# Key eviction per head, 128-wide transposes and reordered statistics in a fused window-attention and Fourier kernel; its constants loaded by fewer transfers on another queue

## The chip, the core and the metric

The kernel runs on one core of a Trainium2 chip. A core has five engines with an instruction queue each. TensorE multiplies matrices (PE in the profile; its loads of the stationary operand are a row of their own, PEld). VectorE (DVE) and ScalarE (ACT) work element by element and can read PSUM, the eight accumulator banks of 2 KB per partition into which TensorE writes. GpSimd (POOL) works on SBUF only. SyncE (SP) issues transfers; ScalarE can issue them too, from the same queue as its arithmetic. Engines wait for each other through semaphores, and each engine takes its instructions strictly in order.

The metric is the device time of one execution in microseconds (us); the median of several runs is compared.

## The reference

Input `x` is 32 images of 56x56 tokens with 128 channels, float32. Two layers are added to it one after the other.

```
x = x + attention(group_norm(x))          # shifted 7x7 windows, 4 heads of 32 channels
x = x + feed_forward(fourier(group_norm(x)))
attention:  q,k,v = win @ w_qkv.T;  softmax(q k^T * scale + bias[h] + mask) v;  @ w_proj.T + b_proj
            bias[h, i, j] = rpb_table[rel_index(i, j), h]      # 49 x 49 per head
fourier:    DCT along one image axis, 32 modes kept, a 128x128 product per mode, inverse DCT;
            the same along the other axis with other weights; the two are added
feed_forward: relu(h @ W1 + b1) @ W2 + b2, 512 hidden channels
```

An image is 8x8 windows of 49 tokens. The windows of one row of windows (392 tokens) are called a row here; there are 256 rows.

## The kernel before

Everything is one software pipeline over **cycles**, one per row, 273 in all. In a cycle, row r starts attention, row r-1 has its softmax divided, row r-2 is transposed, multiplied by its values and projected, and the image before goes through one stage of the Fourier layer or the feed-forward. The order of all work of PE, ACT, DVE and POOL in the loop is written out by hand (the scheduler is off there); the instructions before it, which load constants, are placed by the scheduler. The stage functions of a cycle are called in this order: `full_first`, then `quarters` and `half_columns` (either one first), `eighths`, `full_last`.

In `full_first`, PE transposes the softmax of row r-2 (`attn_transpose`, L393: 8 transposes of 113x113 into two PSUM banks, which DVE copies out at L403 and ACT at L401). Then `attn_qk` makes the queries (L307) and the keys (L312) of row r. ACT evicts the queries (L308). The scores matmul works on two heads at once and needs two copies of the keys: `k_sb[0]` with the channels of the odd heads zero, `k_sb[1]` with those of the even heads zero. ACT writes the first from the keys' bank (L314) and DVE the second (L317); each multiplies by a column of `heads`, ones and zeros per channel, and adds a bias. ACT then squares the row r-3 (L478) and DVE sums it (L480). The feed-forward in (`ff_in`, L670) writes four hidden blocks into four PSUM banks, and ACT evicts them with the ReLU (L678).

PSUM is two pools of four banks: `pa` for attention, `pc` for Fourier and feed-forward. A matmul that takes a bank waits for the eviction of what was there. In four of eight cycles `modes_transpose` (L606, evicted by DVE at L612) takes two `pc` banks just ahead of `ff_in`, whose last two blocks then wait for a bank.

`quarters` has the scores (L347; DVE adds bias and mask at L356) and the inverse transforms (L627). `attn_max` (DVE L366, POOL L367) subtracts the row maximum; ACT takes the exponential later (L373). `eighths` has the values (L415; evicted by ACT L446 and DVE L444). `full_last` has the feed-forward out (L690; DVE L699), the load of three rows of the next image (`image_group`: L243, ACT L253, DVE L254) and the projection (L455; DVE L463). By the row's number within its image, cycles 0 to 7 differ in what Fourier does: row 2 has the statistics (`fourier_stats`: DVE L490 and L498, PE L502, POOL L520) and the width transform (L548, ACT L555), rows 3 and 4 the height transform, row 5 a mix of modes (L585) and no feed-forward, rows 6, 7, 0 and 1 the inverse transforms; all but row 5 have one group of feed-forward.

Ahead of the loop, ACT's queue issues 50 transfers of constants, among them 25 of the 49 rows of the relative position bias `rpb` (L152). SP's queue issues the image, the other 24 rows and one copy of `rpb` onto partitions 64 and up (L153). DVE adds `rpb` and the mask into `bm` (L170), which L356 reads.

Of the kernel before, what the change touches and what calls it, by code (L numbers as in the profile page):

```python
# [15 lines left out]
P = 128  # L16
S = 56
# [31 lines left out]
def swin_fourier_kernel(  # L49
# [68 lines left out]

    def const_load(shape, src, name):
        t = const.tile(shape, F32, tag=name, name=name)  # L120
        nc.scalar.dma_start(t, src)
        return t
# [17 lines left out]
    rpb = const.tile([P, NH, WS, WS], F32, tag="rpb", name="rpb")  # L140
    nc.vector.memset(rpb, 0.0)
    span = 2 * WS - 1
    with nc.allow_non_contiguous_dma(reason="relative position bias, once"):
        for i in range(WT):
            iy, ix = divmod(i, WS)
            src = bass.AP(
                rpb_rev.tensor,
                rpb_rev.offset + (WS - 1 - iy) * span + WS - 1 - ix,
                [[span * span, NH], [span, WS], [1, WS]],
            )  # L150
            eng = nc.sync if i % 2 else nc.scalar
            eng.dma_start(rpb[i : i + 1], src.unsqueeze(0))  # L152
# [4 lines left out]
    for hh in range(2):  # L157
        rows = slice(hh * JP, hh * JP + WT)
        for k, src in enumerate((shift_mask[:, 0, 0:WT], shift_mask[:, 2, JP : JP + WT])):
            nc.scalar.dma_start(mask_sb[rows, :, k], src.rearrange("r p j -> p r j"))  # L160
# [18 lines left out]
    for r in range(0, TC, S):  # L179
        nc.scalar.dma_start(dct_h[r : r + S - SS], dct[r + SS : r + S])  # L180
        nc.scalar.dma_start(dct_h[r + S - SS : r + S], dct[r : r + SS])
# [3 lines left out]
    with nc.allow_non_contiguous_dma(reason="constant, once"):  # L185
        for li, ls in enumerate(HALVES):
            nc.scalar.dma_start(idctw[ls], idct_w[ls, li * 2 * S : (li + 1) * 2 * S])
            src = idct_h.rearrange("p (h r) -> p h r", r=4)[ls, :, 2 * li : 2 * li + 2]
            nc.scalar.dma_start(idcth[ls, : S - SS], src[:, SS:])
            nc.scalar.dma_start(idcth[ls, S - SS :], src[:, :SS])  # L190
# [15 lines left out]

    k_sb = [big.tile([P, NWR, WT], F32, tag=f"k{u}", name=f"k{u}") for u in range(2)]
    heads = const.tile([P, 2], F32, tag="heads", name="heads")
    nc.vector.memset(heads, 0.0)
    for h in range(NH):  # L210
        nc.vector.memset(heads[h * HD : (h + 1) * HD, h % 2 : h % 2 + 1], 1.0)
# [50 lines left out]
    def image_norm(im):  # L262
# [33 lines left out]
        im.bias = small.tile([P, 5], F32, tag="bqkv", name="bqkv")  # L296
        nc.vector.tensor_scalar(im.bias[:, 0:1], pb[:, 0:1], QS, None, ALU.mult)
        nc.vector.tensor_copy(im.bias[:, 1:3], pb[:, 1:3])
        nc.vector.tensor_scalar(im.bias[:, 3:5], heads, im.bias[:, 1:2], None, ALU.mult)
# [3 lines left out]
    def attn_qk(im, i):  # L303

        q, src = q_sb, im.xw[i][:, :RT]
        pq = attn_bank()
        nc.tensor.matmul(pq[:, :RT], lhsT=im.w[:, 0:C], rhs=src, start=True, stop=True)  # L307
        nc.scalar.activation(  # L308
            q[:, :RT], pq[:, :RT], AF.Identity, bias=im.bias[:, 0:1], scale=QS
        )  # L310
        pk = attn_bank()
        nc.tensor.matmul(pk[:, :RT], lhsT=im.w[:, C : 2 * C], rhs=src, start=True, stop=True)  # L312
        pk3 = pk[:, :RT].rearrange("p (w j) -> p w j", j=WT)
        nc.scalar.activation(  # L314
            k_sb[0], pk3, AF.Identity, bias=im.bias[:, 3:4], scale=heads[:, 0:1]
        )
        nc.vector.tensor_scalar(  # L317
            k_sb[1], pk3, heads[:, 1:2], im.bias[:, 4:5], ALU.mult, ALU.add
        )
# [65 lines left out]
    def attn_transpose(im, i, r):  # L385

        a = a_sb[r % 3]
        im.aT = []
        for hf in range(2):
            pt = attn_bank()  # L390
            for m in range(4):
                pr, hp = 2 * hf + m // 2, m % 2
                nc.tensor.transpose(  # L393
                    pt[:PW, m * P : m * P + PW],
                    a[:PW, hp, 2 * pr : 2 * pr + 2].rearrange("p w j -> p (w j)")[:, :PW],
                    ident[:PW, :PW],
                )
            aT = work.tile([P, 4, P], F32, tag="aT", name="aT")
            src = pt[:PW].rearrange("p (m x) -> p m x", x=P)[:, :, :PW]
            if hf:  # L400
                nc.scalar.copy(aT[:PW, :, :PW], src)  # L401
            else:
                nc.vector.tensor_copy(aT[:PW, :, :PW], src)  # L403
            im.aT.append(aT)

    def attn_values(im, i, r):
# [4 lines left out]
        for pr in range(NWR // 2):  # L411
            for h in range(NH):
                for u in range(2):
# [4 lines left out]
                        rhs=im.aT[pr // 2][  # L418
                            ks, 2 * (pr % 2) + h // 2, h % 2 * JP : h % 2 * JP + WT
                        ],  # L420
# [325 lines left out]
    def full_first(cycle, norm):  # L746
# [13 lines left out]
        for im, c in fourier(cycle):  # L760
            if c == 0:
# [5 lines left out]
        for im, c in fourier(cycle):  # L767
            if c in FF_AT:
                ff_in(im, FF_AT.index(c))
        for im, c in fourier(cycle):  # L770
            if c == 0:
                next(im.stats)
# [23 lines left out]
    def quarters(cycle):  # L796
# [3 lines left out]
        for im, c in fourier(cycle):  # L800
            for width, g in back_groups(c):
                modes_back(im, width, g)

# [28 lines left out]
    with tc.manual_schedule(engines={ET.PE, ET.Activation, ET.DVE, ET.Pool}):  # L832
# [6 lines left out]
        for cycle in range(NB * NWR + CONV_BEGIN + FF_AT[-1] - NWR + 1):  # L839
            full_first(cycle, norm)  # L840
            if cycle >= CONV_BEGIN and (cycle - CONV_BEGIN) % NWR != 3:
                quarters(cycle)
                if row(cycle)[0]:
                    attn_max(cycle)
                half_columns(cycle)
                eighths(cycle)
            else:
                half_columns(cycle)
                quarters(cycle)
                eighths(cycle)  # L850
                if row(cycle)[0]:
                    attn_max(cycle)
# [68 lines left out]
```

## Time and profile before

| what | value |
|---|---|
| median of 3 runs | 4120.96 us (4119.18 to 4123.46) |
| the profiled execution | 4120.96 us, its span 4119.1 us |
| mean granted TensorE clock | 0.986 |
| PE busy | 3897.2 us (95%) |
| PEld busy | 3193.5 us (78%) |
| DVE busy | 2336.8 us (57%) |
| ACT busy | 2150.4 us (52%) |
| POOL busy | 1367.1 us (33%) |
| first queries matmul (L307) starts | at 63.62 us |
| DMA engines busy, first 63.6 us | 60% |

The span runs from the first to the last instruction. Busy times are unions per engine; a busy PE is not PE at its peak, since matmuls overlap. A group's row gives line, engine, operation, what it writes and reads, sizes and count, then busy time and the mean of one in ns, then the engine's idle time ahead of it and what ended it. In a timeline a row is: start, length, engine, line, operation, tiles, count, and in brackets the idle time ahead with the releaser. A queue (ACTq, SPq) is the engine issuing a transfer.

### The profile page before, as it was taken

What the parts mean: (1) busy time and instruction counts of PE and PEld (TensorE: products, weight loads), DVE (VectorE), ACT (ScalarE), POOL (GpSimd) and SP (SyncE); (2) the same over time, 40 slices, a digit from 0 to 9 for tenths busy, and PEclk for the clock granted to TensorE, in tenths of its full rate; (3) what the DMA queues carried; (4) which work ended last, traced back from release to release, by engine and by line L of the source; (5) the groups of instructions that cost most, each with busy time, mean ns of one, the idle gap of its engine ahead of it and who ended that gap; (6) DMA issues with size and microseconds to landing.
All of it is one profiled execution on the core that took longest, in us unless ns stands there. A gap on an engine that the chain in (4) does not pass through costs nothing.

```text
span 4119.1 us, 165389 instructions
## 1 busy us (share of the span) xinstructions
PE 3897.2 (95%) x74816; PEld 3193.5 (78%) x74816; DVE 2336.8 (57%) x4859; ACT 2150.4 (52%) x3809; POOL 1367.1 (33%) x1357
## 2 busy tenths in 40 slices
PE   3799999999999999999999999999999999999999
PEld 2577877878777787788777878778778787777887
DVE  3565555665555656555655555565555655556551
ACT  1355555555555555555555555555555555555553
POOL 2333333333333333333333333333333333333321
PEclk9899999999999999999999999999999999999999
DMA  3211222221222221222212222212222212222122
GB/s 90 54 50 51 66 74 75 73 64 47 73 73 74 75 56 54 74 70 77 75 52 57 71 71 78 69 51 61 72 75 73 64 46 73 74 73 75 48 61 62
DMA packets 533828, 273.06 MB, mean 66 GB/s; under 512 B 29795, under 2 KB 532740, under 8 KB 532868
## 3 DMA queue, kind: packets, MB, share of 16 engines
q1 hardware_dynamic: 522072, 257.04, 23.7%
q8 instruction: 588, 9.63, 0.9%
q10 hardware_dynamic: 11052, 5.44, 0.6%
q14 instruction: 116, 0.95, 0.1%
HBM read 159.60 MB, written 102.76 MB: 64 GB/s over the span
## 4 chain that ended last, share of the span: by engine, by line
PE 86%; DVE 6%; ACT 3%; POOL 1%; issue 1%; ACTq 1%; DMA 0%; POOLq 0%; DVEq 0%
PE pc L690 18%; PE pc L670 14%; PE pa L347 7%; PE pa L327 6%; PE pc L585 6%; PE pc L548 5%; PE pa L393 5%; PE pa L415 4%; PE pc L627 4%; PE pa L455 4%; PE pa L307 4%; PE pa L312 4%; PE pc L606 2%; PE pa L243 2%; POOL a L367 1%
## 5 line engine op out<-in xcount | busy, mean ns | idle before, releaser
L381 POOL TENSOR_TENSOR a<-a,rs 128x784 f32<-128x784 f32 x256 | 389.5, 1522 | 1624.3 <-DVE rs L380 1397.2
L690 PE MATMUL pc<-wff,hid 128*128 128x128 f32 (+1 forms) x6400 | 778.8, 279 | 2.0 <-ACT oT L446 0.9
L690 PEld LDWEIGHTS pc<-wff,hid 128*128 128x128 f32 (+1 forms) x6400 | 731.3, 189 | 22.2 <-issue 3.2
L670 PE MATMUL pc<-xf,wff 128*128 128x512 f32 (+2 forms) x1792 | 730.6, 545 | 8.7 <-ACT hid L678 6.4
L678 ACT ACTIVATE hid<-pc,b1sb 128x512 f32<-128x512 f32 (+2 forms) x896 | 559.2, 633 | 181.3 <-PE pc L670 172.5
L670 PEld LDWEIGHTS pc<-xf,wff 128*128 128x128 f32 x1792 | 320.7, 190 | 311.1 <-issue 197.9
L367 POOL TENSOR_TENSOR a<-a,mx 128x784 f32<-128x784 f32 x256 | 388.8, 1519 | 422.5 <-DVE mx L366 409.4
L699 DVE TENSOR_TENSOR res<-pc,res 128x512 f32<-128x512 f32 (+2 forms) x256 | 143.5, 571 | 588.6 <-issue 288.1
L401 ACT COPY aT<-pa 113x452 f32<-113x452 f32 x256 | 138.4, 541 | 547.7 <-PE pa L393 547.7
L317 DVE TENSOR_SCALAR k<-pa,heads,bqkv 128x392 f32<-128x392 f32 x256 | 175.4, 685 | 433.5 <-ACT k L314 433.5
L258 POOL TENSOR_TENSOR xl<-xl,bproj 112x384 f32<-112x384 f32 (+1 forms) x256 | 291.1, 1138 | 291.1 <-PE pa L243 286.3
L347 PEld LDWEIGHTS pa<-k,q 64*64 64x64 f32 x16384 | 266.4, 135 | 131.6 <-issue 58.9
L373 ACT ACTIVATE a<-a 128x784 f32<-128x784 f32 x256 | 221.4, 865 | 253.5 <-POOL a L367 253.5
L356 DVE TENSOR_TENSOR a<-pa,bm 128x392 f32<-128x392 f32 x512 | 260.2, 551 | 162.5 <-PE pa L347 162.2
L444 DVE TENSOR_SCALAR oT<-pa,bqkv 128x147 f32<-128x147 f32 (+2 forms) x768 | 171.2, 280 | 300.3 <-PE pa L415 300.3
L393 PE MATMUL pa<-ident,a 113*113 113x113 f32 x2048 | 259.4, 271 | 84.7 <-ACT xw L253 83.9
L334 ACT COPY v<-pa 128x512 f32<-128x512 f32 x256 | 152.7, 597 | 340.8 <-PE pa L327 340.8
L347 PE MATMUL pa<-k,q 64*64 64x49 f32 x16384 | 300.0, 221 | 10.4 <-ACT k L314 6.2
L393 PEld LDWEIGHTS pa<-ident,a 113*113 113x113 f32 x2048 | 234.2, 185 | 90.9 <-issue 86.6
L660 POOL TENSOR_TENSOR res<-res,b2sb 128x512 f32<-128x512 f32 (+2 forms) x256 | 263.2, 1034 | 97.4 <-DMA res<-scr 86.9
L327 PE MATMUL pa<-wn,xw 128*64 128x128 f32 x4096 | 283.3, 281 | 0.0
L327 PEld LDWEIGHTS pa<-wn,xw 128*64 128x64 f32 x4096 | 221.1, 138 | 46.9 <-issue 20.7
(89 smaller groups left out, 6370.9 us busy)
## 6 DMA issues: line engine op xcount, KB each, us to landing
htok<-scr SPq DMA_DIRECT2D x256, 196.0 KB
res<-scr SPq DMA_DIRECT2D x160, 256.0 KB
out_dram<-res SPq DMA_DIRECT2D x128, 256.0 KB
scr<-xl SPq DMA_DIRECT2D x128, 224.0 KB
xl<-in_x_dram SPq DMA_DIRECT2D x32, 784.0 KB
xl<-in_x_dram SPq DMA_DIRECT2D x32, 672.0 KB
scr<-xl SPq DMA_DIRECT2D x128, 168.0 KB
out_dram<-res SPq DMA_DIRECT2D x96, 128.0 KB
```

Of the source, the lines that this page charges most:

```text
L258: nc.gpsimd.tensor_tensor(piece, piece, bproj.unsqueeze(1).to_broadcast([TC, n1 - n0, C]), ALU.add)
L327: nc.tensor.matmul(pv[w % 2 * JP : (w % 2 + 1) * JP, (w // 2) * C : (w // 2 + 1) * C], lhsT=im.xw[i][:, w * WT : w * WT + JP], rhs=im.w[:, ...
L347: nc.tensor.matmul(ps[hp][u * JP : (u + 1) * JP, w * WT : (w + 1) * WT], lhsT=q[cs, w * WT : w * WT + JP], rhs=k_sb[u][cs, w], start=True, ...
L356: nc.vector.tensor_tensor(a3, ps[hp][:, :RT].rearrange("p (m j) -> p m j", j=WT), bm[:, i // (NWR - 1), hp], ALU.add,)
L367: nc.gpsimd.tensor_tensor(a3, a3, mx.unsqueeze(2).to_broadcast([P, 2 * NWR, WT]), ALU.subtract)
L381: nc.gpsimd.tensor_tensor(a3, a3, rs.unsqueeze(2).to_broadcast([P, 2 * NWR, WT]), ALU.mult)
L393: nc.tensor.transpose(pt[:PW, m * P : m * P + PW], a[:PW, hp, 2 * pr : 2 * pr + 2].rearrange("p w j -> p (w j)")[:, :PW], ident[:PW, :PW],)
L585: nc.tensor.matmul(pz[hs, c * S : (c + 1) * S], lhsT=wmix[:, k, hs], rhs=y[:, k], start=True, stop=True,)
L660: nc.gpsimd.tensor_tensor(res[:m, c0:c1], res[:m, c0:c1], b2sb[:m].unsqueeze(1).to_broadcast([m, c1 - c0, C]), ALU.add,)
L670: nc.tensor.matmul(ph[:, :n], lhsT=wff1[:, f * P : (f + 1) * P], rhs=xff[:, t0 : t0 + n], start=True, stop=True,)
L678: nc.scalar.activation(hf[:, :n], ph[:, :n], AF.Relu, bias=b1sb[:, f : f + 1])
L690: nc.tensor.matmul(pf[:m, c * C : (c + 1) * C], lhsT=im.hid[f][:, c * P : c * P + m], rhs=wff2[:, f], start=(f == 0), stop=(f == NF - 1),)
```

## The change

Six edits are made together.

1. **Position bias.** `rpb` is filled by 7 transfers of one partition each into a helper tile `cols` and 7 transfers from there to `rpb`, in place of 49. Both tiles borrow the two buffers of `zT`.
2. **Queues.** All constants but three (`gavg`, `wqkv`, `bproj`) are issued by SP; ACT keeps these three and three of the seven `cols` transfers.
3. **Keys.** `heads` and its bias columns are gone. Both key tiles are cleared once, and in each row four instructions of 32 partitions write the heads 0, 1, 2, 3: ACT, DVE, ACT, DVE.
4. **Transposes.** `attn_transpose` transposes 128x128 with the padding columns, in place of 113x113, and DVE makes both copies.
5. **Statistics.** The first half of `fourier_stats` comes after `ff_in`, the second half at the end of `quarters`, behind `attn_max`.
6. **Maximum.** `attn_max` is always called at the end of `quarters`; in the cycles that run `half_columns` first (the early ones and each row 5) it came after `eighths`.

```diff
+    FIRST = ("gavg", "wqkv", "bproj")
     def const_load(shape, src, name):
-        nc.scalar.dma_start(t, src)
+        (nc.scalar if name in FIRST else nc.sync).dma_start(t, src)
...
+        cols = work.tile([P, 4, C], F32, tag="zT", name="rpb_cols")...
+        for ix in range(WS):
+            src = bass.AP(rpb_rev.tensor, rpb_rev.offset + WS - 1 - ix, [[span, NH * span], [1, WS]])
+            (nc.scalar if ix % 2 else nc.sync).dma_start(cols[ix : ix + 1]..., src.unsqueeze(0))
+        for iy in range(WS):
+            nc.sync.dma_start(rpb[iy * WS : (iy + 1) * WS], cols[:, :, WS - 1 - iy : span - iy])
...                                # mask, dct_h, idctw, idcth: nc.scalar -> nc.sync
-        nc.scalar.activation(k_sb[0], pk3, AF.Identity, bias=im.bias[:, 3:4], scale=heads[:, 0:1])
-        nc.vector.tensor_scalar(k_sb[1], pk3, heads[:, 1:2], im.bias[:, 4:5], ALU.mult, ALU.add)
+        for h in range(NH):
+            hs = slice(h * HD, (h + 1) * HD)
+            dst = k_sb[h % 2][hs]
+            if h % 2:
+                nc.vector.tensor_scalar(dst, pk3[hs], im.bias[hs, 1:2], None, ALU.add)
+            else:
+                nc.scalar.activation(dst, pk3[hs], AF.Identity, bias=im.bias[hs, 1:2])
...
-                    pt[:PW, m * P : m * P + PW], a[:PW, hp, 2 * pr : 2 * pr + 2]...[:, :PW], ident[:PW, :PW],
+                    pt[:, m * P : (m + 1) * P], a[:, hp, 2 * pr : 2 * pr + 2]..., ident,
-            if hf:
-                nc.scalar.copy(aT[:PW, :, :PW], src)
-            else:
-                nc.vector.tensor_copy(aT[:PW, :, :PW], src)
+            nc.vector.tensor_copy(aT.rearrange("p m a j -> p (m a j)"), pt)
...                                # full_first: ff_in ahead of fourier_stats, its second half taken out
     def quarters(cycle):
...
+        if row(cycle)[0]:
+            attn_max(cycle)
+        for im, c in fourier(cycle):
+            if c == 0:
+                next(im.stats)
...                                # loop: the two calls of attn_max outside quarters are gone
```

## The prediction

> **What bounds the kernel now.** I read the page first: busy time and the chain that ended last.
>
> ```profile
> PE 3897.2 (95%) x74816; PEld 3193.5 (78%) x74816; DVE 2336.8 (57%) x4859; ACT 2150.4 (52%) x3809; POOL 1367.1 (33%) x1357
> PE 86%; DVE 6%; ACT 3%; POOL 1%; issue 1%; ACTq 1%; DMA 0%; POOLq 0%; DVEq 0%
> ```
>
> PE sets the pace, so an edit counts for what it adds to PE or for how long it makes PE wait. Next, the timeline of the start.
>
> ```profile
> 3.15 21.50 ACTq L152 DMA_DIRECT2D rpb<-in_rpb_rev_dram  x25
> 33.73 0.81 SPq L153 DMA_DIRECT2D rpb<-rpb  x1
> 38.84 2.29 DVE L170 TENSOR_TENSOR bm<-rpb,mask 49x343 f32<-49x343 f32 x8 [5.79 <-DMA rpb<-rpb]
> 50.23 2.29 ACTq L121 DMA_DIRECT2D b2sb<-in_b_dram  x1
> 54.38 3.25 PE L243 MATMUL pa<-ident_x,xl 112*128 112x112 f32 x16 [44.17 <-ACT xw L253]
> 63.62 1.66 PE L307 MATMUL pa<-xw,wn 128*128 128x392 f32 x2
> 69.26 1.04 DVE L356 TENSOR_TENSOR a<-pa,bm 128x392 f32<-128x392 f32 x2 [1.24 <-PE pa L347]
> ```
>
> ACT issues transfers until 52.5, and only then evicts the first image; PE waits 44 us. Last, the timeline of one cycle (a row 1 of an image), and the groups.
>
> ```profile
> 1636.24 0.82 PE L312 MATMUL pa<-xw,wn 128*128 128x392 f32 x2
> 1636.90 0.82 PE L606 MATMUL pc<-ident,z 128*128 128x128 f32 x6
> 1637.16 0.68 ACT L314 ACTIVATE k<-pa,bqkv,heads 128x392 f32<-128x392 f32 x1
> 1637.56 3.64 PE L670 MATMUL pc<-xf,wff 128*128 128x512 f32 x8
> 1637.74 0.51 ACT L478 ACTIVATE sq<-xl 112x384 f32<-112x384 f32 x1
> 1637.88 0.69 DVE L317 TENSOR_SCALAR k<-pa,heads,bqkv 128x392 f32<-128x392 f32 x1 [1.80 <-ACT k L314]
> 1638.68 0.69 ACT L678 ACTIVATE hid<-pc,b1sb 128x512 f32<-128x512 f32 x1 [0.43 <-PE pc L670]
> ```
>
> ```profile
> L308 ACT ACTIVATE q<-pa,bqkv 128x392 f32<-128x392 f32 x256 | 150.4, 588 | 41.2 <-PE pa L307 14.6
> L444 DVE TENSOR_SCALAR oT<-pa,bqkv 128x147 f32<-128x147 f32 x256 | 94.8, 370 | 300.3 <-PE pa L415 300.3
> ```
>
> See that DVE's key copy starts when ACT's ends (1637.84, 1637.88), though both only read the bank: they are serial, in all 256 rows. And the first hidden block is evicted as soon as it exists; ACT is 0.43 us ahead of PE there, no more.
>
> **What the Trainium skill says.** "PSUM — Partial Sum Buffer", PSUM bank collisions raise a hardware error: two engines may not touch one bank in one 32-partition quadrant together, reads included; different quadrants may. The four heads are four quadrants, so the chip would allow the four new evictions side by side; but the program's list of waits has each wait for the one ahead of it, as the trace has for the old two. "Vector Engine (DVE) Microarchitecture Reference", Measured stream behaviour on trn2: cost goes by columns, 1.04 ns each plus about 75 on DVE, 0.83 plus about 98 on ACT. So 32 partitions cost as much as 128. The trace agrees on the slope (an L699 of 64 partitions and 128 columns takes 272 ns, of 128 and 256 takes 418: 1.14 per column) and has a larger fixed part. "DMA: Bandwidth & Descriptors", Issuing engines are not separate DMA queues: another issuing engine saves only issue time. Here that time is what ACT lacks. "TensorE: Matmul & The Clock Gate", What's actually happening: a window of about 3.4 us without enough work halves the clock. The trace agrees: at 2583.0 to 2586.4 the granted clock is 0.54.
>
> **The change, part by part.** All sums are on the span of 4119.1, which the profiled execution (4120.96, also the median) exceeds by 1.9.
>
> *Start.* ACT keeps six transfers: three constants took 1.9 us together, three of the bias at 0.86 each (21.50/25) 2.6; it is free at about 5.5, table load until 7. The first image's last transfer is issued at 11.8; all groups are then evicted by about 16, 5 us of norm follow (59.2 to 63.6 before), POOL's eight bias adds end near 20, and the queries start near 21.5. Now the keys: `bm`'s additions stand ahead of DVE's key evictions. SP, after the image at 11.9, issues `wproj` (0.45), four columns (0.7 each), four masks (0.6), then waits for the columns, seven fills (0.7), four `dct` transfers (2), and the copy to partition 64 at about 25. Before, that copy took 5.1 us from issue to `bm`; now this gives 30, `bm` 2.3, the last key eviction 0.6, scores 1: the first L356 near 33.5 against 69.26. **-36 us.** From both sides: -41 if the copy lands in 2 us and a fill costs 0.4, -30 if a fill costs 1.5. The big weights and the second image are issued by about 58, needed after 70: hidden.
>
> *Keys.* Per row, before: 0.68 on ACT, 0.03 handover, 0.69 on DVE, 1.4 in all; ACT is free after 0.57. After: four instructions in a chain. ACT 0.59 (as L308, with no scale column). DVE from L444: 147 columns take 370 ns, 1.04 for each of 245 more, 0.62. Chain 0.59+0.03+0.62+0.03+0.59+0.03+0.62 = 2.5; ACT reaches L478 about 1.75 us after the chain's start, where it took 0.57. So **everything behind it on ACT is 1.2 us later**: L478, then L678. Who waits: PE's last two `ff_in` blocks where L606 has taken two banks. By the list of waits the third block then waits for the first L678 (before: for that or for L612).
>
> - Row 1: PE would start its third block at 1637.56+1.71 = 1639.27, +0.08 for the transposes. The first L678 ends at 1637.16+0.08+1.75+0.42+0.69 = 1640.1. PE waits 0.8: with the transposes **+0.88**.
> - Row 0, likewise with a later start of `ff_in`: **+0.73**.
> - Row 7 (blocks of 256 columns, already waiting 0.19): first L678 0.95 later relative to PE, **+0.8**.
> - Row 6 waits likewise, about +0.9, from which 0.5 of row 5 (below) is taken: **+0.4** for both.
> - Rows 3, 4: four blocks find free banks, scores come 3.4 us later; the chain hides under `ff_in`. Only the transposes: **+0.08** each.
>
> *Transposes.* Eight of 113 take 0.80 us from start to L307's, eight of 128 (L606) 0.88: +0.08 a row, included above. DVE's second copy costs 0.6 of DVE (57% busy) ahead of a key eviction that waits for L312 anyway. If DVE were late by 0.5 more, L612 and L463 would hold PE; about 0.2 a row.
>
> *Statistics, row 2.* L502 now waits for L498 after the scores, which it catches by 0.5, as before. But ACT's first L555 needs POOL's L520, now behind L366 (0.97) on DVE and L367 (1.52) on POOL: 12.6 us into the cycle instead of 8.1. The feed-forward out takes L555's bank at 13.0 and waits to 13.3: **+0.44** with the transposes.
>
> *Maximum, row 5.* L366 moves ahead of L444, so the projection waits 0.9 for L444; but L367, L373 and L253, for which the next transposes wait 2.56 us, come 0.5 earlier.
>
> *Sum.* 0.88+0.73+0.8+0.4+0.16+0.44 = 3.4 us an image; 30 images run with full feed-forward: **+102**. The long wait at row 5 halves the clock afterwards in about half of the images, at some 1.2 us each; broken in two by L455, it does so less often: -8 (0 to -18). The first 16 cycles have no feed-forward to hide the chain: +1.1 a cycle in most, L444 up to 0.9 later in ten, part of it slack: **+14** (6 to 25). Total -36+102-8+14 = **+72: 4121+72 = 4193 us**.
>
> **Rivals.**
>
> 1. *Faster: the chain is hidden.* If the third block never waits, as in rows 3 and 4, the loop pays only transposes (256 x 0.08 = 20 us) and the start's few: -36+20-8+6 = -18, 4103. For it: ACT is 52% busy and waits 172.5 us for L670. Against it: it needs the chain's lag on ACT under 0.43 us in rows 0, 1 and 7, and two handovers with one DVE instruction already cost 0.68. It turns from slower to faster where the loop's stalls fall below about 1 us an image.
> 2. *Slower still: DVE falls behind.* DVE gets about 1.15 us a row. If L612 and L463 come late too, or L555 later, 2 us more an image: 4193+60 = 4253. For it: in rows 0 and 1 DVE runs L699, L463, two copies, two keys, two L612 without a gap. Against it: it idles 40% of the time, just ahead of L444.
> 3. *The start yields less.* `bm` waits on SP's longer queue and nothing of attention ends before it. If the first scores come at 45: 4205.
> 4. *The evictions don't wait for each other.* Then ACT is free after 1.17 instead of 1.75; stalls halve: 4145. The list of waits speaks against it.
>
> **How the numbers follow.** My forecast and the third rival, which is inside it: 0.65, own range 4160 to 4225. Second rival 0.14; fourth 0.08; first 0.13. Less than 0.2% (8 us) is about what a measurement of this kernel can't tell from no change. Of the first rival I give 0.08 to faster (below 4112.7), 0.05 to the same; the rest, 0.87, is slower. The range leaves about 0.1 on each side: 4125 to 4262.
>
> **What would show it.** Right: the queries start near 21 and the first L356 near 33; each row has four key instructions of about 0.6 alternating ACT and DVE; PE shows new waits ahead of L670 released by ACT's L678, some 0.8 us in rows 6, 7, 0 and 1, about 90 us in all; L690 waits for L555 in row 2; ACT's row of idle time names the key of DVE. PE's busy time grows by 20. Wrong: waits on L670 stay near 6 us (rival 1), or PE waits on L612, L463 and L444 for over 60 us (rival 2), or the first L356 comes after 45 (rival 3).

## The result

The changed kernel takes 4236.23 us (median of 4 runs, 4233.28 to 4241.63); the kernel before, on the same chip, 4120.07 (4115.09 to 4123.46). The ratio is 1.0284, with an interval of 1.0267 to 1.0302: slower by 116 us. The forecast was 4193, in a range of 4125 to 4262. The direction and the main mechanism were right, and the loss was 43 us larger than the forecast.

All times below are set against the kernel before as it ran on the same chip; its median there was between 4120 and 4127. Where two changed kernels are compared, their medians are subtracted; set each against the kernel before on its own chip, and these differences come out 4 to 7 us larger, which changes no reading.

### The profile after

The profiled execution took 4241.63 us, its span is 4239.8. In the changed kernel the lines have moved (L307 is L314, L312 is L319, L314 and L317 are L327 and L325, L478 is L480, L670 is L672, L678 is L680). The page first, with busy times and the chain that ended last:

```profile
PE 3946.7 (93%) x74816; PEld 3220.9 (76%) x74816; DVE 2750.1 (65%) x5334; ACT 2126.9 (50%) x3809; POOL 1368.0 (32%) x1359
PE 76%; ACT 10%; DVE 9%; POOL 3%; issue 1%; DMA 0%; ACTq 0%; POOLq 0%; DVEq 0%
```

PE's share of the chain fell from 86% to 76%, ACT's rose from 3% to 10% and DVE's from 6% to 9%: PE now waits for them. Neither ACT nor DVE is near full. The list of waits names the place (columns: engine and work that waited, what it waited for, us in total, times, the longest):

```profile
ACT k L327 <- DVE k L325: 175.8, 256, 0.7
PE pc L672 <- ACT hid L680: 125.5, 119, 1.6
PE pa L401 <- ACT xw L261: 40.7, 33, 1.5
PE pa L457 <- DVE oT L446: 32.9, 34, 3.4
PE pc L692 <- ACT y L557: 17.9, 30, 0.8
```

In the kernel before, the second, third and fourth of these were:

```profile
PE pc L670 <- ACT hid L678: 6.4, 31, 0.6
PE pa L393 <- ACT xw L253: 83.9, 34, 2.9
PE pa L455 <- DVE oT L444: 12.5, 8, 3.3
```

The feed-forward's wait for ACT was 6.4 us before and is 125.5. The wait ahead of the transposes (L401) was 83.9 and is 40.7; in its place stands a part of the wait ahead of L457, 32.9 where it was 12.5. The timeline of the same row 1 as in the prediction:

```profile
1674.71 0.82 PE L319 MATMUL pa<-xw,wn 128*128 128x392 f32 x2
1675.37 0.82 PE L608 MATMUL pc<-ident,z 128*128 128x128 f32 x6
1675.63 0.58 ACT L327 ACTIVATE k<-pa,bqkv 32x392 f32<-32x392 f32 x1
1676.02 1.88 PE L672 MATMUL pc<-xf,wff 128*128 128x512 f32 x4
1676.24 0.62 DVE L325 TENSOR_SCALAR k<-pa,bqkv 32x392 f32<-32x392 f32 x1 [1.11 <-ACT k L327]
1676.89 0.58 ACT L327 ACTIVATE k<-pa,bqkv 32x392 f32<-32x392 f32 x1 [0.69 <-DVE k L325]
1677.50 0.52 ACT L480 ACTIVATE sq<-xl 112x384 f32<-112x384 f32 x1
1677.50 0.63 DVE L325 TENSOR_SCALAR k<-pa,bqkv 32x392 f32<-32x392 f32 x1 [0.65 <-ACT k L327]
1678.04 1.27 ACT L680 ACTIVATE hid<-pc,b1sb 128x512 f32<-128x512 f32 x2
1678.17 1.02 DVE L614 COPY zT<-pc 128x512 f32<-128x512 f32 x2
1678.78 1.98 PE L672 MATMUL pc<-xf,wff 128*128 128x512 f32 x4 [0.88 <-ACT hid L680]
```

The four key instructions form a staircase, ACT, DVE, ACT, DVE; none starts before the one ahead of it has ended. The square (L480) starts 1.87 us after the chain's start, where it took 0.58 before. The first hidden block is evicted from 1678.04 on, and PE, which had finished two blocks of `ff_in` and has no bank for the third, resumes 0.05 us after that eviction's end. The groups confirm the sizes (busy us, mean ns, then idle time ahead and its cause):

```profile
L325 DVE TENSOR_SCALAR k<-pa,bqkv 32x392 f32<-32x392 f32 x512 | 320.7, 626 | 411.2 <-ACT k L327 411.1
L327 ACT ACTIVATE k<-pa,bqkv 32x392 f32<-32x392 f32 x512 | 296.2, 579 | 218.0 <-DVE k L325 175.8
L315 ACT ACTIVATE q<-pa,bqkv 128x392 f32<-128x392 f32 x256 | 150.4, 587 | 694.0 <-PE pa L314 694.0
```

A key instruction of 32 partitions costs ACT 579 ns, and the queries' eviction of 128 partitions costs it 587: working on a quarter of the partitions saved nothing. Last, the timeline of the start:

```profile
2.36 2.92 ACTq L157 DMA_DIRECT2D rpb_cols<-in_rpb_rev_dram  x3
6.93 3.22 PE L251 MATMUL pa<-ident_x,xl 112*128 112x112 f32 x16 [6.93 <-DMA xl<-in_x_dram]
15.20 5.83 SPq L161 DMA_DIRECT2D rpb<-rpb_cols  x7
21.05 1.66 PE L314 MATMUL pa<-xw,wn 128*128 128x392 f32 x2
22.68 0.80 SPq L164 DMA_DIRECT2D rpb<-rpb  x1
25.31 2.29 DVE L181 TENSOR_TENSOR bm<-rpb,mask 49x343 f32<-49x343 f32 x8
29.85 1.04 DVE L364 TENSOR_TENSOR a<-pa,bm 128x392 f32<-128x392 f32 x2 [1.58 <-PE pa L355]
```

ACT is done with transfers at 5.3 us, the queries start at 21.05 instead of 63.62, and the first scores get their bias at 29.85 instead of 69.26.

### Where the time went

Three stretches of the two traces, cut at the starts of the transposes of rows 14 and 254, add up to the difference of the spans (4239.8 - 4119.1 = 120.7 us; it is above the 116 of the medians because the profiled execution of the changed kernel was the longest of its four). Transposes of row 14 start at 235.5 instead of 251.3 (-15.8); from there to those of row 254 it is 3865.2 instead of 3728.4 (+136.8); the rest is 139.1 instead of 139.5 (-0.4). Since the first scores came 39.4 earlier, the first 16 cycles cost 23.6.

The loop by row of the image: mean us from one cycle's transposes to the next cycle's, over the 30 images between, from the traces of the kernels named (the experiments are below).

| kernel | row 0 | 1 | 2 | 3 | 4 | 5 | 6 | 7 | sum |
|---|---|---|---|---|---|---|---|---|---|
| before | 15.28 | 15.03 | 17.34 | 14.73 | 15.25 | 13.80 | 18.15 | 14.69 | 124.3 |
| after | 16.37 | 16.17 | 17.98 | 14.79 | 15.33 | 13.31 | 19.01 | 15.88 | 128.8 |
| keys alone | 16.33 | 16.17 | 18.66 | 14.69 | 15.27 | 13.85 | 19.09 | 15.81 | 129.9 |
| after, old keys | 15.30 | 15.10 | 16.92 | 14.78 | 15.33 | 13.32 | 17.49 | 14.76 | 123.0 |
| after, one handover | 15.73 | 15.53 | 17.99 | 14.81 | 15.32 | 13.29 | 18.16 | 15.22 | 126.1 |
| after, square last | 16.04 | 16.02 | 18.00 | 14.84 | 15.32 | 13.30 | 18.25 | 15.32 | 127.1 |
| after, statistics first | 16.36 | 16.22 | 17.33 | 14.84 | 15.35 | 13.33 | 18.64 | 15.88 | 128.0 |

The loss is in rows 0, 1, 6 and 7, the four in which the inverse transform's transposes take two `pc` banks, and in row 2. Rows 3 and 4, whose `ff_in` finds four free banks, lose under 0.1 though the chain runs there too.

### The profile page after: what moved, and what is told of

It is laid out like the page before. It is cut to its first block, busy times and chain, and to the rows that moved or that the text cites. A ratio compares the mean times of both kernels' runs of the same rounds, so it can differ in the third digit from the quotient of the medians.

```text
span 4239.8 us, 165590 instructions
## 1 busy us (share of the span) xinstructions
PE 3946.7 (93%) x74816; PEld 3220.9 (76%) x74816; DVE 2750.1 (65%) x5334; ACT 2126.9 (50%) x3809; POOL 1368.0 (32%) x1359
## 4 chain that ended last, share of the span: by engine, by line
PE 76%; ACT 10%; DVE 9%; POOL 3%; issue 1%; DMA 0%; ACTq 0%; POOLq 0%; DVEq 0%
PE pc L692 18%; PE pc L672 10%; PE pa L335 6%; PE pc L587 6%; PE pa L355 5%; PE pa L401 5%; ACT k L327 5%; PE pa L457 4%; PE pc L629 4%; PE pa L314 4%; PE pc L550 4%; PE pa L319 3%; PE pa L419 3%; DVE k L325 3%; POOL a L375 2%; ACT hid L680 2%
## 5 line engine op out<-in xcount | busy, mean ns | idle before, releaser
L672 PE MATMUL pc<-xf,wff 128*128 128x512 f32 (+2 forms) x1792 | 744.6, 547 | 125.5 <-ACT hid L680 125.5
L692 PE MATMUL pc<-wff,hid 128*128 128x128 f32 (+1 forms) x6400 | 778.7, 279 | 18.8 <-ACT y L557 17.9
L692 PEld LDWEIGHTS pc<-wff,hid 128*128 128x128 f32 (+1 forms) x6400 | 731.2, 189 | 40.9 <-ACT y L557 22.0
L672 PEld LDWEIGHTS pc<-xf,wff 128*128 128x128 f32 x1792 | 319.6, 190 | 442.8 <-ACT hid L680 201.7
L680 ACT ACTIVATE hid<-pc,b1sb 128x512 f32<-128x512 f32 (+2 forms) x896 | 524.0, 634 | 138.4 <-PE pc L672 132.4
L325 DVE TENSOR_SCALAR k<-pa,bqkv 32x392 f32<-32x392 f32 x512 | 320.7, 626 | 411.2 <-ACT k L327 411.1
L315 ACT ACTIVATE q<-pa,bqkv 128x392 f32<-128x392 f32 x256 | 150.4, 587 | 694.0 <-PE pa L314 694.0
L327 ACT ACTIVATE k<-pa,bqkv 32x392 f32<-32x392 f32 x512 | 296.2, 579 | 218.0 <-DVE k L325 175.8
L407 DVE COPY aT<-pa 128x512 f32<-128x512 f32 x512 | 326.7, 679 | 10.5 <-PE pa L401 10.5
L355 PE MATMUL pa<-k,q 64*64 64x49 f32 x16384 | 310.5, 221 | 18.5 <-DVE k L325 10.2
L401 PE MATMUL pa<-ident,a 128*128 128x128 f32 x2048 | 285.0, 285 | 41.9 <-ACT xw L261 40.7
## 6 DMA issues: line engine op xcount, KB each, us to landing
out_dram<-res SPq DMA_DIRECT2D x96, 128.0 KB
```

Of the source, the lines that this page charges most:

```text
L325: nc.vector.tensor_scalar(dst, pk3[hs], im.bias[hs, 1:2], None, ALU.add)
L327: nc.scalar.activation(dst, pk3[hs], AF.Identity, bias=im.bias[hs, 1:2])
L355: nc.tensor.matmul(ps[hp][u * JP : (u + 1) * JP, w * WT : (w + 1) * WT], lhsT=q[cs, w * WT : w * WT + JP], rhs=k_sb[u][cs, w], start=True, ...
L401: nc.tensor.transpose(pt[:, m * P : (m + 1) * P], a[:, hp, 2 * pr : 2 * pr + 2].rearrange("p w j -> p (w j)"), ident,)
L407: nc.vector.tensor_copy(aT.rearrange("p m a j -> p (m a j)"), pt)
L672: nc.tensor.matmul(ph[:, :n], lhsT=wff1[:, f * P : (f + 1) * P], rhs=xff[:, t0 : t0 + n], start=True, stop=True,)
```

## The experiments

### One part alone

The theory on record: the keys cost, the start gains, the rest is small. Each part was put alone into the kernel before.

**The start alone** (edits 1 and 2).

```diff
+        (nc.scalar if name in FIRST else nc.sync).dma_start(t, src)
...
+            (nc.scalar if ix % 2 else nc.sync).dma_start(
...
+            nc.sync.dma_start(
+                rpb[iy * WS : (iy + 1) * WS], cols[:, :, WS - 1 - iy : span - iy]
```

> The kernel before with the first two edits alone (14 transfers of the bias, the other constants on SP's queue). The theory: what the start gains is kept, since the loop is the same. Between the two profiles the first L356 came 39.4 us earlier (69.26 to 29.85), so 4120 - 39 = 4081 us (4075 to 4088). Rival: the longer SP queue delays the second image or the weights and gives some of it back in the first cycles: 4095 to 4115.

Measured: 4082.37 us, ratio 0.9887 (0.9867 to 0.9907), a gain of 45 us. As expected within the interval.

**The keys alone** (edit 3).

```diff
-        nc.scalar.activation(k_sb[0], pk3, AF.Identity, bias=im.bias[:, 3:4], scale=heads[:, 0:1])
-        nc.vector.tensor_scalar(k_sb[1], pk3, heads[:, 1:2], im.bias[:, 4:5], ALU.mult, ALU.add)
+        for h in range(NH):
+            hs = slice(h * HD, (h + 1) * HD)
+            dst = k_sb[h % 2][hs]
+            if h % 2:
+                nc.vector.tensor_scalar(dst, pk3[hs], im.bias[hs, 1:2], None, ALU.add)
+            else:
+                nc.scalar.activation(dst, pk3[hs], AF.Identity, bias=im.bias[hs, 1:2])
```

> The kernel before with the third edit alone (keys by four instructions of 32 partitions). The theory: the chain ACT, DVE, ACT, DVE keeps ACT's square and first hidden eviction back by 1.2 to 1.3 us, and PE waits for it ahead of the third block in rows 6, 7, 0 and 1: 0.75 to 1.05 us each, 3.7 us an image, 30 images 111 us; the early cycles 15 more: 4246 us (4215 to 4270), with over 90 us of waits of PE on L678's eviction. Rival: it is DVE's whole added load that counts (second copy and keys), then the keys alone, which are half of it, give under 60: below 4180.

Measured: 4309.5 us, ratio 1.044 (1.0424 to 1.0457): 182 us slower, and so outside of the range that was expected. PE's waits in this kernel (here L668 is `ff_in`, L676 its eviction, L500 the matmul of the statistics):

```profile
PE pc L668 <- ACT hid L676: 122.0, 119, 1.5
PE pa L500 <- DVE totc L496: 55.8, 31, 5.1
```

The first line is the wait of the theory, and it is larger than the theory had it (over 90). The second is one that the expectation left out: with the statistics still in their old place, ahead of the scores, row 2's matmul of the column sums waits for a DVE that the chain has delayed (19.5 us in the kernel before, 55.8 here; row 2 takes 18.66 instead of 17.34).

**The statistics alone** (edit 5).

```diff
+            if c in FF_AT:
+                ff_in(im, FF_AT.index(c))
+        for im, c in fourier(cycle):
...
-        for im, c in fourier(cycle):
-            if c == 0:
-                next(im.stats)
...
+                for im, c in fourier(cycle):
+                    if c == 0:
+                        next(im.stats)
```

> The kernel before with the fifth edit alone (first half of the statistics behind ff_in, second half behind quarters and attn_max). The theory: without the key chain DVE has the sums early, PE no longer waits 0.45 us for L498, and the width transform's first eviction comes at 12.3 of the cycle, where L690 starts at 12.4: 32 x 0.45 = 14 us less, 4106 us (4100 to 4118). Rival: the rstd behind POOL's subtraction costs by itself, as the wait of L692 on L557 in the changed kernel suggests: 0.4 to 0.7 more an image, 4133 to 4143.

Measured: 4099.05 us, ratio 0.9934 (0.9917 to 0.9951), a gain of 28 us, more than was expected (the range began at 4100); row 2 takes 16.71 us instead of 17.34, and PE's wait for the column sums is gone from the largest waits.

**The maximum alone** (edit 6).

In the cycles that run `half_columns` first, in the loop:

```diff
-                eighths(cycle)
...
+                eighths(cycle)
```

(the two calls of `attn_max` and `eighths` change places).

> The kernel before with the sixth edit alone (attn_max ahead of eighths in each row 5 and in the early cycles). The theory: POOL's subtraction, the exponential and the image copies, for which the next transposes wait 2.56 us, come 0.5 us earlier (16 us in all), and the half-clock stretches after that wait, in 16 of 30 images at 1.2 us each, get rare (up to 19); the early cycles lose up to 9: 4100 us (4085 to 4108). Rival: the projection's wait for L444 eats it: 4118 to 4130.

Measured: 4092.28 us, ratio 0.9917 (0.9899 to 0.9935), a gain of 35 us, again more than expected. The wait ahead of the transposes falls from 83.9 to 40.6, and that ahead of the projection rises from 12.5 to 32.4; row 5 takes 13.25 instead of 13.80, row 6 17.59 instead of 18.15. Row 6 shows a clock at work: of its 30 passages in the kernel before, 15 take 18.5 to 19.9 us, with a mean granted clock of 0.84 to 0.91, and all but the last of the others 17.5 or 17.6, with a clock of 1.00; here 4 take over 18.2. The traces of the other experiments with the old keys agree: with the maximum in its old place, 13 to 18 of the 30 take over 18.2 (five traces, the kernel before among them), and with it in its new place 2 to 4 (four traces).

**The transposes alone** (edit 4).

```diff
-                    pt[:PW, m * P : m * P + PW],
+                    pt[:, m * P : (m + 1) * P],
...
-            if hf:
-                nc.scalar.copy(aT[:PW, :, :PW], src)
-            else:
-                nc.vector.tensor_copy(aT[:PW, :, :PW], src)
+            nc.vector.tensor_copy(aT.rearrange("p m a j -> p (m a j)"), pt)
```

> The kernel before with the fourth edit alone (transposes of 128, both copies on DVE). The theory: 0.08 us of PE a row and nothing else, since the copies end before the keys: 256 x 0.08 = 21 us, 4141 us (4132 to 4152). Rival: DVE, with 0.6 us more ahead of its key eviction and of L612, falls behind and PE waits for L612, L463 or the keys: 4165 and more.

Measured: 4132.77 us, ratio 1.0021 (1.0014 to 1.0028): some 8 us slower, under half of what was expected. Rows take 0.07 more by the median, row 0 0.03, about as worked out; row 6 is 0.2 shorter in the mean in the profiled execution (17.94), and its passages again lie at about 17.5 or 18.6, so the half-clock stretches take part of the loss back there. Why they fell so was not tested, and one trace does not show that they do so in every execution.

### The keys within the changed kernel

**After, with the old keys.** All of the change but edit 3.

```diff
-        for h in range(NH):
...
+        nc.scalar.activation(
+            k_sb[0], pk3, AF.Identity, bias=im.bias[:, 3:4], scale=heads[:, 0:1]
+        )
+        nc.vector.tensor_scalar(
+            k_sb[1], pk3, heads[:, 1:2], im.bias[:, 4:5], ALU.mult, ALU.add
+        )
```

> The changed kernel with the keys of the kernel before (two products with ones and zeros). The theory: all that is lost comes from the key chain, so -39 (start) + 21 (transposes) - 14 (statistics) - 20 (maximum) against 4120: 4068 us (4050 to 4085). Rival: a good part is DVE's second copy, the statistics or the order: 4100 to 4160.

Measured: 4041.69 us, ratio 0.9796 (0.9782 to 0.9811), below the range that was expected. PE's waits, with `ff_in` at L674:

```profile
PE pa L403 <- ACT xw L263: 41.1, 33, 1.6
PE pa L459 <- DVE oT L448: 31.6, 34, 3.3
PE pc L674 <- ACT hid L682: 5.8, 30, 0.2
```

With the old keys the wait on the hidden block is back at 5.8 us, and the other two waits are as in the changed kernel. So the keys cost 4236 - 4042 = 194 us within the change, and the other five edits together gain 2%. Per image the rows differ by 1.07, 1.07, 1.06 (rows 0, 1, 2), 1.52 (row 6) and 1.12 (row 7).

**After, with one handover.** The heads are evicted in the order 0, 2, 1, 3, so ACT does its two, then DVE its two. The sum of the work is the same, and so is DVE's end.

```diff
-        for h in range(NH):
+        for h in (0, 2, 1, 3):
```

> The changed kernel with the heads evicted in the order 0, 2, 1, 3: the same four instructions on the same engines, but ACT's two follow each other and then DVE's two. The theory: ACT is free 0.65 us earlier in each row (it waits 0.69 for DVE's first), the waits of rows 6, 7, 0 and 1 shrink by as much, 2.6 us an image: 4236 - 79 = 4157 us (4140 to 4175). Rival: it is the number of instructions, or DVE's load, that counts: within 15 of 4236.

Measured: 4157.42 us, ratio 1.0076 (1.0061 to 1.0091), as the theory had it. The same row 1:

```profile
1645.26 1.18 ACT L327 ACTIVATE k<-pa,bqkv 32x392 f32<-32x392 f32 x2
1645.65 1.88 PE L672 MATMUL pc<-xf,wff 128*128 128x512 f32 x4
1646.46 0.52 ACT L480 ACTIVATE sq<-xl 112x384 f32<-112x384 f32 x1
1646.47 1.27 DVE L325 TENSOR_SCALAR k<-pa,bqkv 32x392 f32<-32x392 f32 x2 [1.71 <-ACT k L327]
1647.75 1.98 PE L672 MATMUL pc<-xf,wff 128*128 128x512 f32 x4 [0.22 <-ACT hid L680]
1647.77 1.02 DVE L614 COPY zT<-pc 128x512 f32<-128x512 f32 x2
```

ACT reaches the square after 1.20 us instead of 1.87, and PE's gap falls from 0.88 to 0.22: 0.67 against 0.66. DVE reaches L614 2.51 us after the chain's start, where it was 2.54, so DVE is just as late and PE does not mind. In these rows what counts is the lag on ACT, not the chain's end on DVE: rows 0, 1, 6 and 7 give the whole gain (0.64, 0.64, 0.85 and 0.66 us an image).

Elsewhere it is the other way round. Row 2 stays at 17.99 (17.98), where with the old keys it takes 16.92. There DVE goes without a gap from its last key through the sums, the statistics and the softmax's sum to the bias add of the scores, which starts 8.51 us after the cycle's transposes in this kernel, 8.52 in the changed one and 7.17 with the old keys (medians of the 30 images): it follows the chain's end on DVE, which this order leaves where it was. The early cycles don't gain either: the transposes of row 14 start at 236.8 (235.5; with the old keys 209.8). Between the profiled executions the keys cost 202 us. Of these, by the rows' means, 84 are the alternation, 60 are what two instructions on ACT in place of one still cost in the four rows, 32 are row 2 and 26 the early cycles.

**After, with the square last.** The square and the two sums move behind the four hidden blocks, in all rows but row 2 (in row 1 too, against what the expectation says).

```diff
+        late = all(c % NWR for im, c in fourier(cycle))
-        if im:
+        if im and not late:
             attn_sums(im, i)
...
+        if im and late:
+            attn_sums(im, i)
```

The first pair of lines stands ahead of `ff_in`, the second behind it.

> The kernel after, with the square and the two sums of the attention output put behind the four hidden groups of the feed-forward in every row where nothing needs them early (not in rows 1 and 2, where the last norm and the final sums read them). Theory: what hurts is what stands behind the chain of keys on ScalarE; the square is 0.55 us of it ahead of the first hidden group, so the third block of the feed-forward waits that much less in rows 0, 6 and 7: 3 to 4 rows x 0.55 x 30 = 50 to 66 us, 4170 to 4186 us, ratio about 1.013. Rival: what the block waits for is VectorE, which is late by its own two key instructions and hands over its hidden group late: within 15 us of 4236, ratio 1.025 to 1.03.

Measured: 4189.72 us, ratio 1.0161 (1.0146 to 1.0176): 46 us less than the changed kernel, a little under the 50 to 66 of the theory. PE's waits:

```profile
PE pc L672 <- ACT hid L680: 50.8, 90, 1.0
PE pc L692 <- DVE xf L640: 12.8, 57, 1.2
```

The wait on the hidden block fell by 75 us, more than the gain. Much of the rest was handed on: DVE's sum of the square (L482) now waits 1.61 us in row 1 for the late square, everything behind it on DVE is later, and PE waits at L692 for `xf` in 57 of the 60 rows 0 and 1. Against the changed kernel, rows 6 and 7 are shorter by 0.76 and 0.56, rows 0 and 1 by only 0.33 and 0.15.

**After, with the statistics first.** The second half of the statistics ahead of `attn_max` instead of behind it.

```diff
-        if row(cycle)[0]:
-            attn_max(cycle)
         for im, c in fourier(cycle):
             if c == 0:
                 next(im.stats)
+        if row(cycle)[0]:
+            attn_max(cycle)
```

> The changed kernel with the second half of the statistics ahead of attn_max, not behind it. The theory: rstd no longer stands behind DVE's maximum and POOL's subtraction, the transform's first eviction comes over a microsecond earlier, and PE's wait of 0.6 to 0.7 us at L692 goes: 4236 - 21 = 4215 us (4208 to 4224). Rival: POOL's division (1.52 us) stands in the way all the same, or the maximum, now later, delays the exponential: within 8 of 4236.

Measured: 4216.25 us, ratio 1.0221 (1.0206 to 1.0236), 20 us less and as expected. Row 2 takes 17.33 instead of 17.98. The variance plus epsilon, a DVE instruction on one column (L518), in the changed kernel and then in this one (duration min/median/max in ns):

```profile
L518 DVE SCALAR_TENSOR_TENSOR ve<-nm,ms x32: 159/1406/1412, 160.8 to 4129.1; 128x1 f32<-128x1 f32 x32
```

```profile
L518 DVE SCALAR_TENSOR_TENSOR ve<-nm,ms x32: 159/160/162, 160.0 to 4102.2; 128x1 f32<-128x1 f32 x32
```

The same instruction takes 1.41 us in one order and 0.16 in the other. Row 2 of the changed kernel shows what runs beside it:

```profile
1700.16 1.52 POOL L375 TENSOR_TENSOR a<-a,mx 128x784 f32<-128x784 f32 x1 [0.58 <-PE pc L550]
1700.29 1.40 DVE L518 SCALAR_TENSOR_TENSOR ve<-nm,ms 128x1 f32<-128x1 f32 x1
1701.77 0.55 POOL L522 TENSOR_TENSOR rstd<-ve,mhalf 128x1 f32<-128x1 f32 x1
1702.36 2.26 ACT L557 ACTIVATE y<-pc,rstd 128x448 f32<-128x448 f32 x4 [3.28 <-POOL rstd L522]
1703.07 1.16 PE L692 MATMUL pc<-wff,hid 128*128 128x128 f32 x8 [0.62 <-ACT y L557]
```

L518 starts inside POOL's subtraction and ends with it: 1700.29 + 1.40 = 1701.69, against 1700.16 + 1.52 = 1701.68. In 30 of 32 images its start falls inside such an instruction and its end is a median of 12 ns after POOL's. The Trainium skill has this ("SBUF — State Buffer", Who interferes with whom): a DVE instruction with two inputs from SBUF and a GpSimd instruction that reads SBUF hold each other up, whichever is second waiting for the whole of the first. The trace agrees, and prices it at 1.25 us for L518.

Row 2 does not pay that price, though. L522, which needs L518's result, stands behind the same subtraction on POOL's own queue: POOL is free at 1701.68, L518 ends at 1701.69 and L522 starts at 1701.77, so a quick L518 could have saved it 0.09 us at most. What the other order changes is L522's place: ahead of the subtraction it starts 10.44 us after the cycle's transposes, behind it 12.35 (medians of the 30 images). Row 2 gives 0.65 us an image, 20 us in all. Row 6 is shorter as well, 18.64 instead of 19.01, because only 2 of its passages in this trace, not 11, are slow; no run shows why.

### The change without what costs

To the run of the old keys the old transposes are added; against that run:

```diff
-                    pt[:, m * P : (m + 1) * P],
+                    pt[:PW, m * P : m * P + PW],
...
-            nc.vector.tensor_copy(aT.rearrange("p m a j -> p (m a j)"), pt)
+            if hf:
+                nc.scalar.copy(aT[:PW, :, :PW], src)
+            else:
+                nc.vector.tensor_copy(aT[:PW, :, :PW], src)
```

> The kernel before with the new start, the statistics in two halves and the row maximum taken from PSUM, but with its own keys and its own transposes. Theory (the parts add up once the keys are out): the kernel after with the old keys less what the new transposes cost alone, 4042 - 8.5 = 4033 us, ratio 0.9775 (0.974 to 0.980). Rival: the new transposes cost nothing once the other parts are in: ratio 0.9796 again, 4042 us.

Measured: 4032.91 us, ratio 0.978 (0.9763 to 0.9796). (The maximum is not taken from PSUM, as the expectation has it: it is still made from `a`, only earlier.) Edits 1, 2, 5 and 6 without 3 and 4 give the fastest kernel of the study, 2.2% under the one before; the gap to the old keys with the new transposes, 0.0016, is about the 0.0021 that the transposes cost alone, but the intervals overlap.

The same with the second half of the statistics ahead of the maximum:

```diff
-                if row(cycle)[0]:
-                    attn_max(cycle)
                 for im, c in fourier(cycle):
                     if c == 0:
                         next(im.stats)
+                if row(cycle)[0]:
+                    attn_max(cycle)
```

> The same kernel with the second half of the statistics put ahead of the attention's maximum in the order of work, as in the run of the kernel after where that gave 20 us. Theory: that gain was there because the chain of keys held the statistics up; without the chain row 2's scores wait for little, so it is the same as its neighbour within 6 us (4027 to 4039). Rival: the order matters by itself: 15 to 20 us faster than its neighbour, about 4015.

Measured: 4033.03 us, ratio 0.9781 (0.9766 to 0.9796), the same as its neighbour. L518 takes 1.41 us there and 0.16 here, and the time is the same. The order of statistics and maximum matters only where row 2's path is already late.

### The start, taken apart

In this run the bias comes in 14 transfers, but every other constant stays on ScalarE's queue: edit 1 without edit 2.

Against the run of the start alone:

```diff
-        (nc.scalar if name in FIRST else nc.sync).dma_start(t, src)
+        nc.scalar.dma_start(t, src)
...
-            nc.sync.dma_start(mask_sb[rows, :, k], src.rearrange("r p j -> p r j"))
+            nc.scalar.dma_start(mask_sb[rows, :, k], src.rearrange("r p j -> p r j"))
```

(and the same for `dct_h`, `idctw` and `idcth`).

> The kernel before with the position bias in 14 transfers, and every other constant still issued by ScalarE. Theory (what holds the start is the time ScalarE spends issuing): its 25 transfers of the bias took 21.50 us, the three that stay take 2.9, so it is free 18.6 us earlier, at about 34, and the queries start near 45 instead of 63.6; about half of the gain of the whole start: 4102 us against 4120 (4095 to 4108), ratio 0.9955. Rival: the first row waits for the bias, not for ScalarE, and the 14 transfers alone give the whole gain, 4082. Second rival: the constants that follow on ScalarE wait for the DMA engines and take longer in the emptier time: gain under 8 us.

Measured: 4116.3 us, ratio 0.9976 (0.9966 to 0.9986), a gain of 10 us; the theory's range was missed on the side of its second rival. The start:

```profile
23.18 0.44 ACTq L121 DMA_DIRECT2D w0sb<-in_w_dram  x1
35.95 0.34 ACTq L121 DMA_DIRECT2D wff<-in_W_dram  x1
36.29 0.79 SPq L160 DMA_DIRECT2D rpb<-rpb  x1
36.33 2.27 DVE L177 TENSOR_TENSOR bm<-rpb,mask 49x343 f32<-49x343 f32 x8 [30.44 <-DMA rpb<-rpb_cols]
39.78 1.28 ACT L260 ACT_TABLE_LOAD   x1 [39.78 <-DMA xl<-in_x_dram]
56.85 1.04 DVE L363 TENSOR_TENSOR a<-pa,bm 128x392 f32<-128x392 f32 x2 [1.58 <-PE pa L354]
```

Up to 23.6 ScalarE is ahead as worked out. Then its queue stands still for 12.3 us: the two largest constants (`w1sb`, `w0sb`, 2 MB each) have just been issued, and the next issue comes at 35.95, while the small transfers of the bias land only at 36.3 too (`rpb<-rpb_cols` was issued up to 25.9). ScalarE is free at 39.8 instead of the 34 of the theory, and the first scores come at 56.85: 12.4 us earlier than before, not 18.6. The changed kernel has such a stretch as well, where SP issues `b2sb` for 7.53 us from 35.01 on, but there no eviction stands behind it. What holds the queue is not shown. The large loads are near each pause, but they alone do not set it: in the kernel before, after the same two (issued at 41.85 and 43.39), three more issues followed up to 45.73, and only then came a pause of 4.5 us. So at least two thirds of the start's gain (39.4 at the first scores, 12.4 of it without the move) came only with the move to SP. That move with the old 49 transfers was not run.

## Why the prediction came out as it did

| term | predicted, us | measured, us |
|---|---|---|
| start, to the first scores | -36 | -39.4 |
| loop: keys, transposes, row 2 and clock | +102 - 8 = +94 | +136.8 |
| first 16 cycles | +14 | +23.6 |
| tail | 0 | -0.4 |
| sum, on the span | +72 | +120.7 |

**The start** held. Queries came at 21.05 (21.5), first scores at 29.85 (33.5). The gain was larger because the copy to partition 64 was in use by `bm` 2.6 us after its issue, not 5.1, and was issued at 22.7, not 25. The claim behind it, that ACT's issuing was what lacked, held; the run without the move showed that the price of that issuing is not a sum of single transfers once the queue pauses among them.

**The keys' mechanism** held in each point: four instructions of 0.58 and 0.62 (0.59 and 0.62), alternating, each waiting for the one ahead; the third block of `ff_in` waits for the first hidden eviction in rows 6, 7, 0 and 1, and nothing happens in rows 3 and 4. The term that failed is "**everything behind it on ACT is 1.2 us later**" and the end of the first L678 worked out from it. The step took ACT's instructions as overlapping by 0.1 us, as seen before the change (a key of 0.68, the square 0.58 later). In the chain they don't: the square starts 0.61 after a key of 0.58, and the hidden block 0.54 after the square instead of 0.42. The first hidden block ends at 1.87 + 0.54 + 0.69 = 3.10 us after the chain's start, and 2.86 was taken. In row 1 PE could have started its third block 1.71 after the first, at 1677.73, and started at 1678.78: 1.05 of waiting, where 0.8 was predicted. In rows 0, 1, 6 and 7 the third block starts later after the chain's start by 0.92, 1.05, 1.17 and 1.10 (medians of the 30 images). In all, 125.5 us of wait on L672 where "about 90" was written. Rows 0, 1 and 7 lost 1.09, 1.14 and 1.19 instead of 0.73, 0.88 and 0.80, and row 6 at full clock 1.1 (17.5 to 18.6) instead of 0.9. For row 7 the forecast had the first L678 0.95 later and booked 0.8 without saying why; it ended 1.10 later.

**Row 2** lost 0.64 instead of 0.44. The path was right (maximum, then POOL, then L522, then L557, then L692 waits), but L557 starts 12.93 us into the cycle, where 12.6 was taken, and the wait of L692 was 17.9/30 = 0.6 instead of 0.3. Which step ahead of it was too short, the forecast's text does not show; L518's 1.40 us are not it, as shown above. The forecast booked the loss under the statistics. The runs show that it takes the keys too: with the new statistics and the old keys row 2 takes 16.92, less than the 17.34 before.

**The maximum** was under-rated. The forecast took 0.5 us an image and 8 us of clock, 23 in all; alone it gained 35. Its two parts (0.55 in row 5, 0.56 in row 6) are about 17 us each. The first is the 0.5 of the forecast; the second, put down there to the clock, is twice the 8 us: 15 slow passages of row 6 became 4, where the wait was expected to spare fewer. In the changed kernel, where row 6 has the keys' wait as well, the clock came out about as forecast: 11 of its 30 passages take 19.6 to 19.9 (granted clock 0.91 or 0.92) and the others about 18.6, so the slow ones add 12 us in all, where in the kernel before they added 22.

**The transposes** were 0.08 a row in the forecast and 0.07 in most rows in their own run; PE's busy time, though, grew by 49.5 in all and not by 20: the transposes' own line by 25.6 (259.4 to 285.0), and lines without any more work too, `ff_in` by 14.0 and the scores by 10.5. It is a poor witness for such a term.

**The first 16 cycles** cost 23.6. With the old keys the transposes of row 14 start at 209.8 instead of 235.5, so all of it, and 2 us more, is the keys'; 1.7 times the 14 that were taken, and inside their range of 6 to 25.

**The rivals.** That the chain is hidden (the first, 4103) fell with 125.5 us of wait. The second (DVE falls behind, 4253) is nearer in its number than the forecast. In rows 0, 1, 6 and 7 its cause is not there: the wait of L319 for DVE's L465 is 6.0 us, as before (6.1), no wait on L614 shows among PE's largest, and with one handover PE gained all of ACT's 0.67 us while DVE stayed as late as it was. In row 2 DVE's lateness does cost, 32 of the keys' 202 us, and the clause on a later L557 came true there; the 26 of the early cycles did not fall with one handover either. The third (the start yields less) fell with the first scores at 29.85. The fourth (evictions don't wait for each other) fell with ACT's wait of 0.69 us for DVE's key in all 256 rows.

What stays open: whether the four evictions would run side by side if the program let them (no run here removed the program's wait between them), and what makes an issuing queue pause near the large loads.

## What to carry to other kernels

Splitting an eviction by partitions buys no time per instruction (579 ns for 32 partitions, 587 for 128), and if the parts alternate between two engines on one bank, each handover adds its partner's full length to the queue behind: price such an edit by what stands behind it on each engine, and if it must be, do one engine's share first (some 80 us here for a change of order). Ask it for each engine and each stage: four rows paid for the lag on ACT, one paid for the chain's end on DVE. Constants are better issued by a queue on which nothing urgent follows. When an order is changed, look at what already stands ahead on each engine's own queue before blaming an instruction that has become long: L518's 1.25 us more cost nothing behind a busy POOL.

## What the runs showed that was not expected

- A DVE instruction on one column took 1.41 us instead of 0.16 while POOL ran beside it, and ended with POOL's instruction. The kernel before has it too, in L285 (median 1222 ns, least 160), where PE waited for it once, 1.9 us. In neither place did it set the time.
- After two loads of 2 MB the next issue on their queue came 12.3 us later in one kernel, and transfers of 5.4 KB each, issued on another queue up to 25.9 us, landed only at 36.3, about when that queue went on.
- Row 6 after its wait takes either about 17.5 us or 18.5 to 19.9 in the kernel before; shortening the wait ahead of it from 2.56 to about 1.25 us made the longer one rarer (15 of 30 to 4 of 30). The longer passages have a granted clock of 0.84 to 0.91, the others of 1.00.
